# A graph network's edge counts: one-hot products on TensorE in place of one scatter per edge

## The chip, the cores and the metric

The kernel runs on one core of a Trainium2 chip. The core has five engines with instruction streams of their own, which wait for each other through semaphores: TensorE (PE: matrix products, with weight loads shown apart as PEld), VectorE (DVE), ScalarE (ACT), GpSimd (POOL) and SyncE (SP, which here only starts DMAs). Sixteen DMA engines move data between HBM and the on-chip memory SBUF; products land in PSUM. DMAs are started from the queues of SP, ACT and POOL. A POOL DMA may be indirect: a column of indices says which rows it reads or writes. The metric is the device time of one execution in microseconds. A measurement of this kernel can tell about 0.2% from no change.

## The reference

There are 6,250 nodes with 128 features and 106,250 directed edges (`src`, `dst`), sorted by `dst`. Four graph blocks follow each other, each with a residual and a layer norm (`_layernorm(x + block(x))`, in shortened form):

```python
agg = segment_sum(h[src], dst); agg /= maximum(deg, 1)        # block 0, twice (SAGE)
out = agg @ Wl.T + bl + h @ Wr.T
out = segment_sum((x @ W)[src] * (dinv[src] * dinv[dst]), dst)  # block 1 once, block 2 twice (GCN, with loops)
for l in range(3):                                             # block 3: three layers of three hops
    for k in range(1, 4): x_k = segment_sum(x_k1[src] * edge_norm, dst)
```

The nine hops weigh each edge by `edge_weight` and by the weighted degrees of its ends; the other five sums only count edges. What matters here: all these sums run over the same edges, and the first five need, for each pair of a destination and a source, only the number of edges between them.

## The kernel before

Nodes are cut into 49 windows of 128 (`NW`). The kernel makes dense matrices in HBM: `counts`, one byte for each pair of source and destination, 39 MB; and `weights`, four bytes for each pair, for the first 34 windows of destinations or so. Columns (destinations) are grouped into 13 chunks of four or three windows (`SHAPE`, 512 or 384 columns); chunk `c` holds 49 blocks of 128 sources. A sum over edges is then a matrix product: for each block of sources, the block of features is the stationary operand and 128 x 512 counts are the moving one.

The work goes through these stages.

Setup (lines 217 to 358) reads `dst`, `src` and `edge_weight`, spread over partitions; makes a key for each edge from its destination and source; writes `keys`, `recs` (rows of 17 edges) and `edges` to HBM; and decides on tests of the edges' order (`odd`) whether `usual_way` can be taken. The other branch, `general_way`, is for inputs of another shape.

Pass 1 (lines 779 to 821) is the first SAGE layer. For each chunk, it

- fetches rows of 17 x 128 edges (`fetch`), compares each edge's key with its 48 neighbours on both sides to find how often the pair occurs and whether the edge is the first of its pair (`cell`, on DVE), and gets a byte address for each edge;
- scatters one byte for each edge into `counts` (`scatter`, line 588: 17 indirect DMAs for each of 49 blocks), after the chunk has been filled with zeros (`empty`);
- counts degrees by one-hots of 384 places and products (`degrees`, lines 730 to 732), and turns them into the norms (`norms`);
- sums: `counted_sum` (line 479) loads seven blocks of counts at a time (`columns`, line 462), widens them from bytes to 32 bits, in pass 1 on ACT alone (line 501), and multiplies (line 508). Features are split into a high and a low part, so there are two products for each block. For chunks after the first, a second accumulator `half` takes the layer's output for sources that are already done, which is a part of the next layer's sum;
- does the chunk's dense layer (`mean_conv`, `plus_product`), and splits the result for later use.

From chunk 7 on, further parts of the next layer's sums are made ahead (`early_parts`).

Pass 2 (lines 907 to 919) is the second SAGE layer, with the rest of its sums; passes 3 and 4 (lines 940 to 984) are the GCN blocks. Their counts are widened by DVE and ACT in turn. Meanwhile POOL scatters the weights, 35 blocks of 17 indirect DMAs, paced by the products (`Paced`), and then gathers edge records for the last windows (`gathered_edges`). The hops (from line 1253) multiply by `weights` for most chunks and gather rows for the rest, in an order written out by hand.

Up to the hops, the order on each engine comes from a scheduler that follows the program order and the waits. Two orders are forced: `in_line` puts POOL's DMAs behind each other, and SP starts its DMAs in one line, so that a DMA that waits holds those behind it.

The counts' address and value in the lines that the change removes:

```python
nc.vector.tensor_scalar_add(cval[:, i, :], f1[:], 1.0)
...
ins = nc.gpsimd.indirect_dma_start(
    out=mat[:], out_offset=bass.IndirectOffsetOnAxis(ap=celli[:, i, k:k + 1], axis=0),
    in_=vals[:, i, k:k + 1], in_offset=None, **bounds).ins
```

Of the kernel before, what the change touches and what calls it, by code (L numbers as in the profile page):

```python
# [47 lines left out]
P = 128  # L48
# [39 lines left out]

SLOTS, LOADS, STEP, HOTS, GROUP = 30, 12, 2, 5, 4
# [47 lines left out]
def load_weights(nc, a, const, work, ps, ident, tags):  # L137
# [18 lines left out]
    transposed("w1l", a["L0_gnn_W1l"])  # L156
    transposed("w1r", a["L0_gnn_W1r"])
    transposed("w2l", a["L0_gnn_W2l"])
    transposed("w2r", a["L0_gnn_W2r"])
    bcast("b1l", a["L0_gnn_b1l"], D)  # L160
    bcast("b2l", a["L0_gnn_b2l"], D)
# [22 lines left out]
def kernel(ctx: ExitStack, tc: tile.TileContext, a: dict, out: bass.AP):  # L184
# [15 lines left out]
    counts = dram.tile([BASE[NC] + 4 * NB * KD * P, 1], U8, name="counts")  # L200
# [6 lines left out]
    def empty(mats, dt, c, engine):  # L207
        n = 7 * width(c) // (4 if dt == U8 else 16)
        z = zeros[:].bitcast(dt)[:, :n]
        ins = fills[dt, c] = engine.dma_start(  # L210
            mats[BASE[c]:BASE[c + 1]].rearrange("(p s f) o -> p s (f o)", p=P, f=n),
            z.unsqueeze(1).to_broadcast([P, NW * width(c) // n, n])).ins
        tc.declare_no_dep(ins, group=f"cells {dt}", reason="another chunk")
        tc.add_to_no_dep_group(f"cells {dt}", ins)
        return ins

    with tc.tile_pool(name="setup", bufs=1) as setup, \
            tc.tile_pool(name="ps_setup", bufs=2, space=PSUM) as ps:

        def spread(name, ap, dt):  # L220
            t = setup.tile([P, L + 2 * J], dt, name=name)
            nc.sync.dma_start(t[:], bass.AP(ap.tensor, ap.offset, [[L, P], [1, L + 2 * J]]))
            return t
# [4 lines left out]
        dsti = spread("dsti", a["dst"], I32)  # L228
# [3 lines left out]
        main = slice(J, J + L)  # L232


# [3 lines left out]
        nc.vector.tensor_scalar(k1[:], dsti[:], 1023, 13, op0=ALU.bitwise_and, op1=ALU.logical_shift_left)  # L238
        nc.vector.tensor_scalar(k2[:], dsti[:], 20, 23, op0=ALU.logical_shift_right, op1=ALU.logical_shift_left)
# [5 lines left out]
        nc.sync.dma_start(keys[J:].rearrange("(p e) o -> p (e o)", p=P), key[:, main])  # L245


        def field(at):
# [18 lines left out]
        empty(counts, U8, 0, nc.sync)  # L267

# [7 lines left out]
        dst = setup.tile([P, L + 2 * J], F32, name="dst")  # L276
# [6 lines left out]
        nc.vector.tensor_sub(t1[:], dst[:, 2 * J:2 * J + L], dst[:, main])  # L283
        nc.vector.tensor_scalar(t2[:], dst[:, main], float(NOWHERE), None, op0=ALU.is_lt)
        nc.vector.scalar_tensor_tensor(t2[:], t1[:], 0.0, t2[:], op0=ALU.is_equal, op1=ALU.mult)
        nc.vector.tensor_reduce(odd[:, 1:2], t2[:], AX.X, ALU.max)
        nc.vector.tensor_scalar(t2[:], t1[:], float(NOWHERE // 2), None, op0=ALU.is_lt)
        nc.vector.scalar_tensor_tensor(t2[:], t1[:], 1024.0, t2[:], op0=ALU.is_ge, op1=ALU.mult)
        nc.vector.tensor_reduce(odd[:, 2:3], t2[:], AX.X, ALU.max)
# [3 lines left out]
        dmax = setup.tile([P, RPP], F32, name="dmax")  # L293
        nc.vector.tensor_reduce(dmin[:], by_row(dst[:, main]), AX.X, ALU.min)
        nc.vector.tensor_reduce(dmax[:], by_row(dst[:, main]), AX.X, ALU.max)
        rowi = setup.tile([P, RPP], I32, name="rowi")
        nc.gpsimd.iota(rowi[:], pattern=[[1, RPP]], base=0, channel_multiplier=RPP)
        nc.vector.tensor_scalar(rowi[:], rowi[:], ~(P - 1), None, op0=ALU.bitwise_and)
        even = setup.tile([P, RPP], F32, name="even")
        nc.vector.tensor_copy(even[:], rowi[:])  # L300
        d1 = setup.tile([P, RPP], F32, name="d1")
        d2 = setup.tile([P, RPP], F32, name="d2")
        nc.vector.tensor_sub(d1[:], dmax[:], even[:])
        nc.vector.tensor_scalar(d1[:], d1[:], float(2 * P), None, op0=ALU.is_ge)
# [3 lines left out]
        nc.vector.tensor_sub(d2[:], dmin[:], even[:])  # L308
        nc.vector.tensor_scalar(d2[:], d2[:], -float(P), None, op0=ALU.is_lt)
# [6 lines left out]
        row = setup.tile([P, RPP], F32, name="row")  # L316
        nc.gpsimd.iota(row[:], pattern=[[1, RPP]], base=1, channel_multiplier=RPP,
                       allow_small_or_imprecise_dtypes=True)
# [43 lines left out]
    with tc.If(go == 1) as fork:  # L362
        usual_way(tc, a, out, dram, ident, part, first, over, keys, recs, edges, counts, weights, fills, empty)
# [5 lines left out]
def usual_way(ctx, tc, a, out, dram, ident, part, first, over, keys, recs, edges, counts, weights, fills, empty):  # L369
# [9 lines left out]
    iota = const.tile([P, NEAR * P], F16, name="iota")  # L379
    nc.gpsimd.iota(iota[:], pattern=[[1, NEAR * P]], base=0, channel_multiplier=0,  # L380
# [8 lines left out]
    dinvw2 = const.tile([P, NW], F32, name="dinvw2")  # L389

    early_pool = tc.tile_pool(name="early", bufs=1, side="right")
    early = early_pool.__enter__()
    stacked = early.tile([P, DH], F32, name="stacked")
    nc.vector.tensor_add(stacked[:], ident[:, :DH], ident[:, DH:])
    wt = load_weights(nc, a, early, work, ps, ident, ("y", "pp"))

    def new(name, n, d=D):
        return work.tile([P, n, d], F32, name=name, tag=name)


    def table(name, room, dt=F32):
# [1216 lines left out]
```

## Time and profile before

| | us |
|---|---|
| median of 3 runs | 5791.16 (5787.49 to 5791.88) |
| the profiled execution's own time | 5791.37 |
| its span | 5789.5 |
| PE busy | 5254.7 (91%) |
| POOL busy | 4158.4 (72%) |
| DVE busy | 3115.3 (54%) |
| ACT busy | 2141.4 (37%) |
| first product of pass 1 | at 163.46 |
| first product of pass 2 | at 1203.04 |
| first product of the hops | at 2184.53 |

The slices below cut the span into 40 equal parts of 145 us; each digit is the busy share of a slice in tenths, for PEclk the clock that TensorE was granted in tenths of its full speed.

```profile
PE   0656579799999899999999999999999999999998
DVE  7685455258855564444446554444456544444566
ACT  1323346347755442323333323323333333233332
POOL 5777777778877617767767767767777677777775
PEclk9878789899999999999999999999999999999999
DMA  5768785146544449999999999999999999999997
```

Lines of groups read: line of the kernel, engine, operation, what is written and read, its size, the count; then busy time and the mean of one in ns; then the idle time of the engine just before, and what ended it. Lines of waits name who waited for whom, the time in total, how often, and the longest. Lines of the timeline give start and length in us. An engine's busy time does not say that it is the bound of a stage; that is read from what its instructions wait for.

### The profile page before, as it was taken

How to read it: one execution, taken by the hardware profiler on the slowest of the kernel's cores; microseconds unless marked ns; L12 is line 12 of the kernel's file. 1: busy time of each engine (PE TensorE's matmuls, PEld its weight loads, DVE VectorE, ACT ScalarE, POOL GpSimd, SP SyncE). 2: the span in 40 equal slices, each digit the busy share in tenths (PEclk: the TensorE clock that was granted, in tenths of full speed). 3: DMA queues.
4: the chain of work that ended last, by engine and by line, in shares of the span. 5: the costliest groups of instructions: out<-in, count | busy, mean ns of one | idle time of the engine just before them, and what ended most of it. 6: DMA issues, size and time to landing. Idle time of an engine off the chain costs nothing.

```text
span 5789.5 us, 70572 instructions
## 1 busy us (share of the span) xinstructions
PE 5254.7 (91%) x19487; PEld 3143.9 (54%) x19487; DVE 3115.3 (54%) x8828; ACT 2141.4 (37%) x4433; POOL 4158.4 (72%) x4204
## 2 busy tenths in 40 slices
PE   0656579799999899999999999999999999999998
PEld 0334457576788784555555555555555555555455
DVE  7685455258855564444446554444456544444566
ACT  1323346347755442323333323323333333233332
POOL 5777777778877617767767767767777677777775
PEclk9878789899999999999999999999999999999999
DMA  5768785146544449999999999999999999999997
GB/s 184 237 201 248 217 260 154 59 140 177 155 131 137 129 139 333 323 319 325 324 318 310 309 313 323 322 321 323 323 302 312 301 326 324 316 323 324 304 336 264
DMA packets 707889, 1517.46 MB, mean 262 GB/s; under 512 B 153094, under 2 KB 359962, under 8 KB 707226
## 3 DMA queue, kind: packets, MB, share of 16 engines
q1 hardware_dynamic: 524642, 1272.39, 65.1%
q0 software_dynamic: 134080, 180.02, 11.5%
q10 hardware_dynamic: 48760, 60.45, 3.1%
q8 instruction: 155, 2.54, 0.2%
q14 instruction: 252, 2.06, 0.1%
HBM read 1313.22 MB, written 199.20 MB: 261 GB/s over the span
## 4 chain that ended last, share of the span: by engine, by line
PE 71%; DMA 11%; POOL 7%; DVE 6%; issue 4%; ACT 1%; ACTq 0%; SPq 0%; POOLq 0%; DVEq 0%
PE acc L1245 45%; PE acc L508 14%; DMA rows<-stored,gsrc 7%; PE gacc L1212 5%; POOL counts L588 5%; PE pp L435 3%; PE pd L732 1%; DMA cols<-counts 1%; POOL weights L588 1%; PE half L508 1%; DMA slots<-counts 1%; DVE widev L501 1%; DMA counts<-cval,celli 1%; ACT wides L501 1%; POOL rows L1148 1%
## 5 line engine op out<-in xcount | busy, mean ns | idle before, releaser
L1245 PE MATMUL acc<-weighed,hop 128*128 128x512 f32 (+1 forms) x7154 | 3402.6, 591 | 13.2 <-DMA weighed<-weights 6.8
L1148 POOL DMA_INDIRECT rows<-stored,gsrc x2727 | 2614.1, 959 | 981.9 <-issue 347.5
L1195 ACT ACTIVATE both<-rows,gwgt 128x128 fp32r<-128x128 f32 x2718 | 1047.8, 400 | 1969.7 <-DMA rows<-stored,gsrc 1783.5
L1212 PE MATMUL gacc<-both,oh 128*128 128x256 f32 x2718 | 1761.2, 657 | 7.9 <-DVE both L1196 7.9
L1245 PEld LDWEIGHTS acc<-weighed,hop 128*128 128x128 f32 x7154 | 1169.7, 190 | 941.2 <-issue 837.6
L1196 DVE SCALAR_TENSOR_TENSOR both<-rows,gwgt,both 128x128 fp32r<-128x128 f32 x2718 | 923.8, 350 | 1334.1 <-ACT both L1195 1323.6
L508 PE MATMUL acc<-wides,t 128*128 128x512 f32 (+1 forms) x3083 | 875.7, 394 | 359.2 <-ACT wides L501 240.3
L588 POOL DMA_INDIRECT counts<-cval,celli x833 | 828.6, 995 | 263.0 <-issue 245.1
L1212 PEld LDWEIGHTS gacc<-both,oh 128*128 128x128 f32 x2718 | 514.6, 190 | 651.8 <-issue 396.2
L508 PEld LDWEIGHTS acc<-wides,t 128*128 128x128 f32 x3083 | 569.8, 191 | 496.9 <-ACT wides L501 267.1
L588 POOL DMA_INDIRECT weights<-wval,celli x595 | 677.2, 1138 | 181.4 <-issue 167.1
L501 ACT CAST wides<-slots 128x1024 fp32r<-128x1024 uint8 (+3 forms) x684 | 562.3, 862 | 521.5 <-DMA slots<-counts 309.2
L508 PE MATMUL acc<-widev,t 128*128 128x512 f32 (+1 forms) x2044 | 576.8, 390 | 31.5 <-DVE widev L501 27.0
L1175 DVE TENSOR_TENSOR oh<-places,gdst 128x640 fp32r<-128x640 f32 x604 | 473.3, 784 | 213.1 <-PE gacc L1212 212.2
L508 PEld LDWEIGHTS acc<-widev,t 128*128 128x128 f32 x2044 | 376.8, 190 | 112.9 <-DVE widev L501 42.8
L731 DVE TENSOR_SCALAR oh<-iota,dloc 128x384 bf16<-128x384 f16 x833 | 214.2, 320 | 366.8 <-PE pd L732 366.7
L501 ACT CAST wides<-cols 128x1024 fp32r<-128x1024 uint8 (+1 forms) x364 | 285.0, 797 | 298.5 <-DMA cols<-counts 160.7
L501 DVE CAST widev<-cols 128x1024 fp32r<-128x1024 uint8 (+1 forms) x364 | 249.8, 691 | 175.2 <-PE acc L508 137.5
L508 PE MATMUL half<-wides,t 128*128 128x512 f32 (+1 forms) x606 | 188.6, 390 | 0.0
L732 PE MATMUL pd<-oh,lw 128*4 128x384 bf16 x833 | 175.4, 334 | 10.1 <-DVE oh L731 8.1
L501 DVE CAST widev<-slots 128x1024 fp32r<-128x1024 uint8 (+3 forms) x239 | 155.8, 669 | 18.2 <-PE acc L508 13.0
L1065 DVE TENSOR_TENSOR y<-pp,dinvw 128x256 f32<-128x256 f32 (+2 forms) x153 | 82.4, 539 | 139.0 <-PE pp L435 138.7
(266 smaller groups left out, 2790.4 us busy)
## 6 DMA issues: line engine op xcount, KB each, us to landing
weighed<-weights SPq DMA_DIRECT2D x1728, 512.0 KB
weights<-zeros SPq DMA_DIRECT2D x8, 12544.0 KB
slots<-counts SPq DMA_DIRECT2D x174, 448.0 KB
cols<-counts SPq DMA_DIRECT2D x140, 448.0 KB
rows<-stored,gsrc POOLq DMA_INDIRECT x2727
counts<-zeros SPq DMA_DIRECT2D x10, 3136.0 KB
weighed<-weights SPq DMA_DIRECT2D x96, 256.0 KB
stored<-hop ACTq DMA_DIRECT2D x74, 256.0 KB
```

Source lines behind the costliest of these rows:

```text
L435: nc.tensor.matmul(pm[:, j * d:(j + 1) * d], xt[:, j * P:(j + 1) * P], w, start=True, stop=True)
L501: copy(wide[:, :n * cw], t[:, r * cw:(r + n) * cw])
L508: product = nc.tensor.matmul(into[:, :cw], lhs, cols, start=s == begin and i == 0, stop=s == end - 1 and i == len(lhss) - 1).ins
L588: ins = nc.gpsimd.indirect_dma_start(out=mat[:], out_offset=bass.IndirectOffsetOnAxis(ap=celli[:, i, k:k + 1], axis=0), in_=vals[:, i, k:k ...
L731: nc.vector.tensor_scalar(oh[:], iota[:], dloc[:, k:k + 1], None, op0=ALU.is_equal)
L732: nc.tensor.matmul(acc[:], lw[:, k, :], oh[:], start=k == 0, stop=k == KD - 1)
L1148: nc.gpsimd.indirect_dma_start(out=fetched_rows[:, self.slot(self.asked), :], out_offset=None, in_=stored[self.h % 2][:], in_offset=bass.I ...
L1175: nc.vector.tensor_tensor(oh[:, :m, :], places[:].unsqueeze(1).to_broadcast([P, m, P]), gdst[:, i, ks].unsqueeze(2).to_broadcast([P, m, P] ...
L1195: nc.scalar.activation(both[:, :D], x, AF.Copy, scale=w)
L1196: nc.vector.scalar_tensor_tensor(both[:, D:], x, w, both[:, :D].bitcast(F32), op0=ALU.mult, op1=ALU.subtract)
L1212: nc.tensor.matmul(self.acc[:, j * 2 * D:(j + 1) * 2 * D], oh, both, start=k == 0, stop=k == KG - 1)
L1245: nc.tensor.matmul(acc[:, :cw], tables[h][:, s, :], t[:, s % STEP * cw:(s % STEP + 1) * cw], start=s == 0, stop=s == NW - 1)
```

## The change

The matrix of counts is no longer scattered into. The edges are sorted by destination, so the edges of four neighbouring nodes (`G = 4`) lie in one run of at most 128 edges. Setup finds for each four nodes the row of 17 edges where its run begins (`lasts`, `around`, `begin`), and writes `runs`, an overlapping table of 128 keys and 128 edge weights for each row. In pass 1, for each batch of four windows (128 groups), one indirect DMA gathers the runs, one for each partition (`gathered_run`); `prepared` turns keys into a zone (node within the group, source block) and a place (source within the block), transposes them so that edges lie on partitions, and makes the degrees and norms. `building` then makes, for each pair of groups, one-hots of zones (196) and places (128) with one DVE instruction each for eight groups, two products of 128 x 196, and one ACT copy from PSUM into bytes, which writes runs of eight bytes (two groups of four nodes) at a step of 128. A finished window is written to HBM by one DMA.

`building` is a generator. Five windows and one pair are made ahead; after that `Meanwhile` takes 64/49 pairs for each block of sources that `counted_sum` consumes, and in the same way the fills of `weights`, which are now cut into 63 DMAs of 16 pieces for each partition.

Cells are computed only for the 35 blocks that the weights need, at the end of each chunk of pass 1 (three blocks), and their scatters follow at once; `Paced` and the scatter of counts go, as does the counting of degrees. One operand of the cells' comparisons, which was copied to PSUM (`aside`), stays in SBUF. Counts are stored window by window, so a load of seven blocks consists of 896-byte pieces, and the widening copies reorder them. `cols` slots in pass 1 go from seven to five, `wide` buffers from three to two. Weights that only later passes need are loaded after pass 1, and `kept` is allocated there.

```diff
-    def empty(mats, dt, c, engine):
...
+    def empty(c):
+        n = 7 * width(c) // 16
+        mat = weights[BASE[c]:BASE[c + 1]].rearrange("(p s f) o -> p s (f o)", p=P, f=n)
+        fills[c] = []
+        for s in range(0, NW * width(c) // n, 16):
+            ins = nc.sync.dma_start(mat[:, s:s + 16, :], zeros[:, :n].unsqueeze(1).to_broadcast([P, 16, n])).ins
...
+            yield
...
+        nc.scalar.dma_start(lasts[DRIFT:DRIFT + P * RPP].rearrange("(p r) o -> p (r o)", p=P), rowlast[:])
...
+        nc.scalar.dma_start(around[:], bass.AP(lasts.tensor, lasts.offset, [[G, P], [P * G, NBATCH], [1, 2 * DRIFT]]))
+        nc.scalar.dma_start(runs[:, RUN:], bass.AP(a["edge_weight"].tensor, a["edge_weight"].offset + J,
+                                                    [[KD, NW * P], [1, RUN]]))
...
+        for r in (slice(0, 5 * P), slice(5 * P, NW * P)):
+            nc.sync.dma_start(runs[r, :RUN], bass.AP(keys.tensor, keys.offset + J + r.start * KD,
+                                                     [[KD, r.stop - r.start], [1, RUN]]))
...
+    def count_columns(t, c, step, s0):
+        n = SHAPE[c]
+        t = t[:, :n * step * P].rearrange("p (w s f) -> p w s f", s=step, f=P)
+        nc.sync.dma_start(t.rearrange("p w s f -> p w (s f)"), counts[c].rearrange(
+            "(w p f) o -> p w (f o)", w=n, p=P)[:, :, s0 * P:(s0 + step) * P])
+        return t
...
-                copy(wide[:, :n * cw], t[:, r * cw:(r + n) * cw])
+                copy(wide[:, :n * cw].rearrange("p (s w f) -> p s w f", s=n, f=P),
+                     t[:, :, r:r + n, :].rearrange("p w s f -> p s w f"))
...
+            if meanwhile is not None:
+                meanwhile()
...
+        def gathered_run(b):
+
+            t = cells.tile([P, 2 * RUN], F32, name="run", bufs=3)
+            ins = nc.gpsimd.indirect_dma_start(
+                out=t[:], out_offset=None, in_=runs[:],
+                in_offset=bass.IndirectOffsetOnAxis(ap=begin[:, b:b + 1], axis=0)).ins
+            queue.append(in_line(ins))
+            return t
...
+        SOME = 8
+
+        def hot(name, places, spots, k0, n):
+
+            t = hots.tile([P, SOME // 2, n, 2], BF16, name=name)
+            nc.vector.tensor_tensor(
+                t[:], places[:].unsqueeze(1).to_broadcast([P, SOME // 2, n, 2]),
+                spots[:, k0:k0 + SOME].rearrange("p (j o) -> p j o", o=2).unsqueeze(2).to_broadcast(
+                    [P, SOME // 2, n, 2]), op=ALU.is_equal)
+            return t
...
+        def building():
+
+            found, spots = {}, {}
+            found[0] = gathered_run(0)
+            for w in range(NW):
+                b, c = w // WPB, chunk_of(w)
+                if w % WPB == 0:
+                    if b + 1 < NBATCH:
+                        found[b + 1] = gathered_run(b + 1)
+                    spots[b] = prepared(b, found.pop(b))
+                t = spare if w % 2 else cells.tile([P, NW * P], U8, name="built")[:]
+                by_column = t.rearrange("p (s f) -> p s f", f=P)
+                for some in range(GROUPS_W // SOME):
+                    k0 = w % WPB * GROUPS_W + some * SOME
+                    zone = hot("zone", zones2, spots[b], k0, NZ)
+                    place = hot("place", places2, spots[b], P + k0, P)
+                    for pair in range(SOME // 2):
+                        acc = ps_build.tile([P, 2, CW // 2], F32, name="some")
+                        for i in range(2):
+                            nc.tensor.matmul(acc[:, i, :NZ], place[:, pair, :, i], zone[:, pair, :, i],
+                                             start=True, stop=True)
+                        f = some * SOME * G + pair * 2 * G
+                        nc.scalar.copy(by_column[:, :, f:f + 2 * G].rearrange("p s (i d) -> p s i d", d=G),
+                                       acc[:, :, :NZ].rearrange("p i (s d) -> p s i d", d=G))
+                        yield
+                nc.sync.dma_start(counts[c].rearrange("(w p f) o -> w p (f o)", w=SHAPE[c], p=P)[w - START[c]], t)
...
+        meanwhile = Meanwhile()
+        meanwhile.add(building(), 4 * PAIRS_W / NW)
+        meanwhile.some(0, 5 * PAIRS_W + 1)
...
+        meanwhile.add(filling, (ND + 1) * FILLS / (NW * 11))
...
-            fetch_chunk(c + 2)
-            if c + 4 < NC:
-                empty(counts, U8, c + 4, nc.sync)
-            count_cells(c + 1)
-            for i in sorted(i for i in blocks_near(c) if i in degs):
-                degrees(i)
-            norms(c)
...
-            acc = counted_sum(counted, c, both(t0hi, t0lo), [(2, "s")], slots=slots, also=also)
+            acc = counted_sum(counted, c, both(t0hi, t0lo), [(2, "s")], wide_bufs=2, slots=slots, also=also,
+                              meanwhile=meanwhile)
...
-            if c <= ND:
-                empty(weights, F32, c, nc.sync)
+            for i in dense[PER * c:PER * (c + 1)]:
+                filled(chunks_near(i))
+                cell(i, fetch(i))
+        meanwhile.rest()
```

## The prediction

> **What bounds the kernel now.** I read the page's slices first, then the busy time by stage, then the groups and waits of the first stage, then single instructions. The stages come from the timeline: the first product of pass 1 starts at 163.46 us, the first of pass 2 at 1203.04, the first hop product at 2184.53. Busy time in these stretches (columns: stretch, length, busy us and count of PE, weight loads, DVE, ACT, POOL, then granted clock, DMA share, GB/s):
>
> ```profile
> 0.00:163.00 163.00, 2.88 (x7) 1.36 (x7) 103.23 (x323) 15.98 (x26) 92.98 (x104) 1.00 0.55 170
> 163.00:1205.00 1042.00, 755.12 (x3527) 524.26 (x3528) 549.93 (x2119) 439.45 (x586) 797.21 (x804) 0.86 0.63 193
> 1205.00:2180.00 975.00, 924.24 (x4417) 749.83 (x4416) 674.45 (x1640) 529.17 (x760) 654.05 (x570) 0.98 0.52 150
> 2180.00:5789.00 3609.00, 3572.44 (x11538) 1868.49 (x11538) 1787.68 (x4748) 1156.77 (x3062) 2614.12 (x2727) 0.99 0.93 317
> ```
>
> Passes 2 to 4 and the hops are PE's (95% and 99% busy). Pass 1 isn't: PE is at 72% with a clock of 0.86. Its groups and waits, from 40 to 1215 us:
>
> ```profile
> L588 POOL DMA_INDIRECT counts<-cval,celli x833 | 828.6, 995 | 263.0 <-issue 245.1 <-DVE wval L712 9.4 <-DMA counts<-cval,celli 3.7
> L501 ACT CAST wides<-slots 128x1024 fp32r<-128x1024 uint8 x273 | 272.7, 1044 | 380.5 <-DMA slots<-counts 309.2 <-PE half L508 58.2 <-PE acc L508 5.5
> L731 DVE TENSOR_SCALAR oh<-iota,dloc 128x384 bf16<-128x384 f16 x833 | 214.2, 320 | 366.8 <-PE pd L732 366.7
> L732 PE MATMUL pd<-oh,lw 128*4 128x384 bf16 x833 | 175.4, 334 | 10.1 <-DVE oh L731 8.1 <-ACT degT L734 1.7
> L679 DVE TENSOR_TENSOR before<-m,aside 128x816 bf16<-128x816 f32 x48 | 47.7, 994 | 0.1
> L522 ACT COPY agg<-acc 128x512 f32<-128x512 f32 x11 | 6.4, 583 | 9.4 <-PE acc L508 9.4
> L734 ACT COPY degT<-pd 4x384 f32<-4x384 f32 x49 | 22.9, 468 | 159.3 <-PE pd L732 138.2 <-DVE oh L731 19.9 <-DMA slots<-counts 1.2
> L563 DVE TENSOR_TENSOR y<-pp,invdeg 128x384 f32<-128x384 f32 x3 | 1.7, 558 | 1.8 <-PE pp L435 1.8
> ```
>
> The 833 count scatters leave POOL no gap but issue: 828.6 + 263.0 = 1091.6 us, 1.3 us each. ACT waits 309 us for count columns, which are read only when their scatters have landed. So POOL sets pass 1. The scatters end here:
>
> ```profile
> 1124.70 1.04 POOL L588 DMA_INDIRECT counts<-cval,celli  x1 [0.30 <-issue]
> 1126.05 1.07 POOL L588 DMA_INDIRECT counts<-cval,celli  x1 [0.30 <-issue]
> 1127.42 1.00 POOL L588 DMA_INDIRECT weights<-wval,celli  x1 [0.31 <-issue]
> ```
>
> after which the last chunk takes to 1203.
>
> **The change, part by part.** Pass 1 consumes 781 columns of counts ("steps"): 13 chunks of 49, and 144 in the early sums. 81 of 784 build pairs stand ahead of the first step; the rest go at 64/49 = 1.306 a step, so they end after 703/1.306 = 538 steps, in chunk 8. The fills of the weights are spread over the same steps. I price the start, the building steps, the steps after them, and the later passes.
>
> *Start.* Gone: the first count fills, cells and scatters. New: a copy of edge weights and of keys into `runs` (6,272 pieces of 512 B each), the writing and reading back of `lasts`, a gather, `prepared`, 64 pairs before chunk 0 can be read. ACT's queue (60.45 MB, 48,760 packets, 3.1% of 16 engines, so 0.059 us a packet) prices one copy at 6,272/16 x 0.059 = 23 us; `lasts` stands behind it on that queue, and DVE's setup behind `around`. So the branch moves from 34 to about 46 us, the first one-hots to about 53; 16 pairs of one-hots and 64 evictions beside the splits of x take 40; writing and reading back 5 + 4. That is 102; I take 115 for order and queues, and 100 to 163.46 (no gain) as ends.
>
> *ACT in a building step.* Casts: 447 instructions, 389 us by the four forms of L501, over 781 steps 0.50. Evictions, 392 elements from PSUM: L734 (384) 0.468 and L522 (512) 0.583 give 0.475, x 1.306 = 0.62. Short runs can cost more: the writes of single 4-byte cells 12 B apart took 1.35 us for 850 elements (L270), where 17-cell runs took 0.95 (L251). At 1.37 ns an element plus 0.18 an eviction would be 0.72, the upper end; runs of 8 are nearer to the long ones, so 0.475. The rest of ACT (sums, transposes, splits: 53 us) 0.07. Together 1.19.
>
> *DVE.* Gone: L731 (214 us), the degrees' small operations, 14 of 49 cells. New: 196 pairs of one-hots, 1,568 and 1,024 elements, all operands 16-bit. Upper end, by two-source rows (0.682 at 512, 0.994 at 816: 1.03 ns an element): 1.75 + 1.20 = 2.95 a pair. Lower: L731 is the one row with only 16-bit tensors, 0.320 at 384 against 0.558 for the two-source 4-byte form of that size (L563), 0.573 of it: 1.69. I take 1.69 for the type, though L731 has one source. It is 1.69/4 x 1.306 = 0.55 a step. Cells, 35 x 5.6 us (five large at 0.92, ten small at 0.1) over 538: 0.36. `prepared` 11 x 5 us: 0.10; the chunks' ends 0.09. Together 1.10.
>
> The Trainium skill ("VectorE: DVE Perf Modes", The perf-mode tier table) has `tensor_tensor` at twice the rate when everything is bf16 in SBUF, which no row of before shows; with its two elements a cycle the pair would be about 1.65 us and the sum the same within 10 us.
>
> *PE.* Products up to chunk 8: 1,378 at 0.2336 (72 in 16.82 us), narrower ones less: 315 us. Builds: 1,406 at 0.09 (196 of 384 columns of L732, 17 in 2.88 us) to 0.28 (plus L508's 0.19 weight load, unhidden); L435, 128 columns behind a 128x128 load, runs 8 in 1.16, 0.145: I take 0.15, 211 us. L732 goes. Chunk ends 40. 566/538 = 1.05.
>
> *DMA.* Between 800 and 900 us, at 0.98 busy, 295 GB/s moved. Bytes beside the building: fills 112 MB, counts written 35 (the zero fills of counts, 39 MB, go), columns read 35, the rest 15: 197 MB, 670 us, 1.245 a step. The fills come in 1.8 MB parts (6 us each) in SP's queue between count writes and column reads, in place of 12.5 MB at a time; a column read queued behind a part is covered by five slots, an eviction into the second-next `built` by one window's time, 15 us.
>
> *POOL.* 51 weight scatters a chunk at 1.3 us: 1.35 a step. Only the gather of a later run waits behind them in line, with about two chunks of slack; hidden as long as a scatter stays under some 1.8 us. Beside a busy DVE it got longer: 81.86 us for 60 from 1400 to 1500 us, 1.36 each and 0.3 between. The skill ("SBUF — State Buffer", SBUF: two separate sides) speaks against the change: a DVE operation with two SBUF inputs shuts out a GpSimd one that reads SBUF for its whole length, and one-hots and cells now have both inputs in SBUF. If each scatter waited for one 0.97 us one-hot, 2.3 us each would be 2.4 a step; I stay at the row.
>
> *Sum of pass 1.* DMA is the largest, 1.245; ACT, DVE and PE stand close beside it, in fixed orders that wait for each other. Pass 2 to 4 show what such a bound reaches: 865 us of PE work (3,561 products, 80 us of small ones) in 975, 0.89. So 1.245/0.89 = 1.40, x 538 = 753. The 243 steps after have no building: 790 products, 342 of 384 columns at 0.175 and 448 at 0.2336, 165 us, and four chunk ends of 8: 195. Pass 1 ends at 115 + 753 + 195 = 1063 in place of 1203: -140.
>
> *Passes 2 to 4 and hops.* Weight scatters are done about 240 us into pass 2 (187 left of 595), so the one long stall goes:
>
> ```profile
> 1975.93 1.18 PE L508 MATMUL acc<-wides,t 128*128 128x512 f32 x4
> 1991.78 2.07 PE L508 MATMUL acc<-widev,t 128*128 128x512 f32 x4 [14.68 <-DVE widev L501]
> ```
>
> There DVE's casts stood behind gathers behind the last scatters: -14. Columns are read in pieces of 896 B instead of 3,584: some 23 reads lie open at 3.4 us; bounds 0 to +0.9 each, taken +0.2: +4. In the passes with two `cols` buffers a tile takes PE 3.27 us, the cycle of cast and read (1.7 + 3.4)/2 = 2.6: covered up to a read of 4.8; at 5.2 it would cost 0.2 on 182 reads, +36. The late weights load beside the first chunk's products: 0. Hops unchanged: 0. Sum -10.
>
> 5789.5 - 150 = 5639.5 of span, and the 1.9 us that lie around it in that execution (5791.37, against a median of 5791.16): **5641**.
>
> **Rivals.** *All engines overlap almost fully:* start 100, 1.19 a step, chunk ends half hidden: 100 + 640 + 180 = 920, so 5498. For it: the products and builds are data-independent between chunks. Against: chunk ends tie PE, ACT and DVE together.
> *One-hots at the two-source rate (2.95), slower:* DVE 1.10 + 0.41 = 1.51, /0.89 = 1.70, x 538 = 914, start +20, end 1244: +41 - 10, so 5822. It decides from a step of (1203 + 10 - 310)/538 = 1.68. For it: every two-source row of before runs at that rate.
> *Evictions at 0.72:* ACT 1.51, 1.70 a step: about 5816. For it: L270.
> *The count columns' pieces or the casts from four windows slow passes 2 to 4:* +36 to +100, 5680 to 5740 with the gain of pass 1.
> *The built path isn't taken:* dst and the edges' runs in the reference's inputs stay inside the new limits (drift of -2 to 21 rows against 48), so no.
>
> **How the numbers follow.** My case (5540 to 5740, passes 2 to 4 a little slower included) 0.63; near full overlap 0.17; one-hots slow 0.12; evictions slow 0.08, a part of which the drift of the step could still hold at no change. Measurement tells 0.2% (12 us) apart. Faster 0.63 + 0.17 - 0.02 = 0.78, same 0.04, slower 0.18. The range, 5500 to 5820, leaves out about half of the fast and of the slow cases.
>
> **What would show it.** Right: no count scatters, 595 + 13 indirect DMAs on POOL ahead of the edge gathers; pass 2 starting near 1060; a zone one-hot near 1.0 us and a place near 0.7; evictions near 0.475; DMA share above 0.85 up to chunk 8; the 14.68 us stall gone. Wrong: zone at 1.75; evictions above 0.7; scatters above 1.8 with one-hots waiting for a gathered run; column reads above 4.8 us in passes 3 and 4; DVE casts of 1,024 above 0.69.

## The result, and the profile after

The changed kernel takes 5844.94 us (median of 4 runs, 5842.29 to 5850.64) beside 5790.8 us for the kernel before: a ratio of 1.0096, with an interval of 1.0078 to 1.0113. It is slower by about 1%, clear of what a measurement can tell, where I had forecast 5641 and a gain. The profiled execution took 5842.29 us with a span of 5840.4.

The busy slices of the changed kernel's page (145 us each, tenths):

```profile
PE   4646456889999999999999999999999999999999
DVE  7646355628955664444446654444456544444566
ACT  5646456755855443332333323333333333333332
POOL 0654644760000015776767767767777677777775
PEclk9878778999999999999999999999999999999999
DMA  8756656445644558999999999999999899999997
```

From the second to the seventh slice no engine is busy throughout: PE, DVE, ACT, POOL and DMA all stand at three to seven tenths. Sevens alone do not clear an engine: before the change POOL showed sevens all through pass 1 and was its bound, since the rest of its time there was issue, 0.30 us between one scatter and the next. But now POOL too falls to four to six, so the engines seem to take turns waiting. The waits have to show it. The stages, cut at the first product of each (pass 1 at 122.98 us, pass 2 at 1292.57, the steady hop products at 2240.08; columns as before: stretch, length, PE, weight loads, DVE, ACT, POOL, clock, DMA share, GB/s):

```profile
0.00:123.00 123.00, 44.87 (x195) 26.17 (x195) 83.51 (x192) 55.27 (x113) 11.19 (x26) 1.00 0.84 276
123.00:1292.00 1169.00, 771.67 (x4068) 540.14 (x4069) 592.18 (x1312) 693.81 (x1235) 664.60 (x607) 0.85 0.58 174
1292.00:2240.00 948.00, 905.33 (x4407) 747.43 (x4405) 654.28 (x1635) 525.73 (x759) 33.44 (x33) 0.99 0.55 154
2240.00:5840.00 3600.00, 3564.71 (x11538) 1862.09 (x11538) 1786.04 (x4747) 1161.94 (x3062) 2612.26 (x2727) 1.00 0.93 317
```

Pass 2 starts 89.5 us later than before (1292.6 against 1203.0). Passes 2 to 4 take 947.5 us in place of 981.5, 34.0 less; the hops 4.7 less. 89.5 - 34.0 - 4.7 = 50.8, the whole difference of the spans. So the loss lies ahead of pass 2. Pass 1 starts 40.5 us sooner than before (122.98 against 163.46) and still ends 89.5 later, and its waits name the reason. First DVE's, then POOL's (that one from 200 to 900 us):

```profile
DVE ki L760 <- DMA run<-runs,begin: 323.5, 8, 43.8
DVE zone L812 <- PE some L848: 56.9, 62, 3.2
```

```profile
POOL weights L630 <- DVE low L737: 121.8, 4, 31.1
POOL weights L630 <- DVE f L719: 41.0, 1, 41.0
POOL weights L630 <- DVE celli L738: 23.2, 1, 23.2
```

Eight times DVE waits at L760, the first instruction of `prepared`, for a gathered run, 323.5 us in all; and POOL, which issues the gathers, waits for DVE's cells in turn. One round of it in the timeline, POOL first and then DVE:

```profile
422.41 0.98 POOL L630 DMA_INDIRECT weights<-wval,celli  x1 [0.30 <-issue]
423.70 0.99 POOL L748 DMA_INDIRECT run<-runs,begin  x1 [0.31 <-issue]
454.38 1.68 POOL L630 DMA_INDIRECT weights<-wval,celli  x1 [29.68 <-DVE low L737]
```

```profile
426.50 0.23 DVE L760 CAST ki<-run 128x128 int32<-128x128 f32 x1 [35.55 <-DMA run<-runs,begin]
```

The gather at 423.70 is POOL's next instruction after 51 scatters without a pause. Its run lands at 426.5 and DVE goes on after 35.6 us of nothing. Then DVE needs 28 us until the next block's cells are done (454.38), POOL scatters 51 times up to its next gather at 523.83 (69.4 us, 1.36 us each), the gathered run lands 3 us later, and DVE is waiting again. 28 + 69 + 3 is 100, and a chunk of pass 1 takes 100.5 (L607's multiplication, once a chunk, moves from 171.1 to 874.4 in seven chunks). The loop is the bound; the granted clock falls with it, to 0.79 to 0.84 between 200 and 800 us.

### The profile page after: what moved, and what is told of

Its sections match the earlier page's. It is cut to its first block, busy times and chain, and to the rows that moved or that the text cites. A ratio compares the mean times of both kernels' runs of the same rounds, so it can differ in the third digit from the quotient of the medians.

```text
span 5840.4 us, 70939 instructions
## 1 busy us (share of the span) xinstructions
PE 5286.6 (91%) x20205; PEld 3175.8 (54%) x20205; DVE 3116.0 (53%) x7884; ACT 2436.8 (42%) x5168; POOL 3321.5 (57%) x3393
## 4 chain that ended last, share of the span: by engine, by line
PE 57%; DMA 18%; issue 8%; DVE 7%; POOL 6%; ACT 4%; ACTq 0%; POOLq 0%; SPq 0%; DVEq 0%
PE acc L1361 36%; DMA rows<-stored,gsrc 14%; PE acc L552 11%; POOL weights L630 5%; PE gacc L1328 4%; PE pp L467 3%; ACT wides L544 2%; DMA cols<-counts 2%; POOL rows L1264 1%; PE half L552 1%; DVE widev L544 1%; DVE both L1312 1%; ACT both L1311 1%; DVE zone L812 1%; PE some L848 1%
## 5 line engine op out<-in xcount | busy, mean ns | idle before, releaser
L552 PE MATMUL acc<-wides,t 128*128 128x512 f32 (+1 forms) x3083 | 976.0, 408 | 63.1 <-ACT wides L544 56.5
L630 POOL DMA_INDIRECT weights<-wval,celli x595 | 653.6, 1098 | 549.6 <-DVE celli L738 208.3
L544 ACT CAST wides<-slots 128x1024 fp32r<-128x1024 uint8 (+3 forms) x684 | 592.5, 881 | 224.9 <-PE half L552 87.3
L1291 DVE TENSOR_TENSOR oh<-places,gdst 128x640 fp32r<-128x640 f32 x604 | 473.0, 783 | 187.9 <-PE gacc L1328 186.9
L848 PE MATMUL some<-zone,place 128*128 128x196 bf16 x1568 | 273.6, 269 | 301.3 <-DVE place L812 280.3
L986 POOL DMA_INDIRECT gm<-recs,gat x17 | 17.6, 1035 | 880.6 <-DVE gwgt L1003 878.0
L848 PEld LDWEIGHTS <-place 128*128 128x128 bf16 x1568 | 117.5, 104 | 449.1 <-DVE place L812 285.9
L851 ACT CAST built<-some 128x392 uint8<-128x392 f32 x400 | 185.4, 521 | 167.4 <-PE some L848 165.1
L851 ACT CAST slots<-some 128x392 uint8<-128x392 f32 x384 | 177.5, 513 | 141.6 <-PE some L848 137.2
L812 DVE TENSOR_TENSOR zone<-zones,spots 128x1568 bf16<-128x1568 bf16 x196 | 190.0, 969 | 58.0 <-PE some L848 56.9
```

The lines of the kernel that those rows point to most:

```text
L544: copy(wide[:, :n * cw].rearrange("p (s w f) -> p s w f", s=n, f=P), t[:, :, r:r + n, :].rearrange("p w s f -> p s w f"))
L552: nc.tensor.matmul(into[:, :cw], lhs, cols, start=s == begin and i == 0, stop=s == end - 1 and i == len(lhss) - 1)
L630: ins = nc.gpsimd.indirect_dma_start(out=weights[:], out_offset=bass.IndirectOffsetOnAxis(ap=celli[:, i, k:k + 1], axis=0), in_=wval[:, i, ...
L812: nc.vector.tensor_tensor(t[:], places[:].unsqueeze(1).to_broadcast([P, SOME // 2, n, 2]), spots[:, k0:k0 + SOME].rearrange("p (j o) -> p ...
L848: nc.tensor.matmul(acc[:, i, :NZ], place[:, pair, :, i], zone[:, pair, :, i], start=True, stop=True)
L851: nc.scalar.copy(by_column[:, :, f:f + 2 * G].rearrange("p s (i d) -> p s i d", d=G), acc[:, :, :NZ].rearrange("p i (s d) -> p s i d", d=G))
```

## The experiments

**Chips.** The runs fell on several chips, and these are of two kinds. On some, as on the chip of the result, before takes 5788 to 5796 us. On others it takes 7800 to 7913 us, and the changed kernel 6927. In the experiments a kernel is compared with kernels on the same kind of chip. What differs is told at the end of this section. Where a chunk is given, it is the mean of chunks 1 to 7 of pass 1, from the starts of L607's multiplication.

**The run gathered earlier.** My theory after the result: the place of the gather in POOL's line makes the loss. The edit of the run with six buffers (`e1`; `c2`, `c3` and `c4` are the same kernel):

```diff
-            t = cells.tile([P, 2 * RUN], F32, name="run", bufs=3)
+            t = cells.tile([P, 2 * RUN], F32, name="run", bufs=6)
...
-            found[0] = gathered_run(0)
+            for b in range(4):
+                found[b] = gathered_run(b)
...
-                    if b + 1 < NBATCH:
-                        found[b + 1] = gathered_run(b + 1)
+                    if b + 4 < NBATCH:
+                        found[b + 4] = gathered_run(b + 4)
```

With four buffers (`e2`, `c5`) two runs are gathered ahead, and then `b + 2`. In what follows, "theory" is this account, and "rival" is another one that an experiment could bring out.

> The gather of each run is issued one batch earlier (four buffers in place of three), so it stands in front of 51 more weight scatters in POOL's queue. Theory (the loss is DVE's in-line read of a run whose gather stands behind 51 scatters, eight stalls of 33 to 44 us, 324 us in all): the waits of L760 go, a chunk of pass 1 takes 60 to 68 us in place of 100 (its running part is 60; POOL's 51 scatters and one gather are 51 x 1.29 + 2.8 = 68), and the time is 5844 - 8 x (32 to 41) = 5516 to 5590. Rival A (the engines share ports and DMA so that a step costs 1.40 us, my sum): a chunk 69 plus its end, about 5640. Rival B (DVE or POOL are late for another reason, the cells for instance, and the run is only what the wait shows): 5780 to 5850.

> The same with six buffers: each run is gathered three batches earlier. Theory: no stall is left that one batch did not already take, so within 20 us of the run with one batch earlier. If the first of the two leaves a part of the stalls (DVE's order could read the run still earlier), this one takes it, and is the faster by that part.

Both were on a chip of the slower kind (before 7800). Four buffers: 6911 us, 0.8842 of before [0.8797, 0.8888], a chunk of 103.0. Six buffers: 6861, 0.8797 [0.8748, 0.8845], 94.1. With four buffers L760 still waited three times in pass 1, 95.7 us in all. The built order says why: DVE's read of a run moved forward with the gather. Most runs had been read 1.25 to 1.44 batches ahead of their own one-hots, and were now read 2.25 to 2.44 ahead, so the batch of lead was used up at once. Six buffers leave the read at 2.3 to 2.5. With them the waits of L760 went, but pauses of 15 to 36 us stood in their place, for which the profile names no engine of this core; some of them ended as POOL's burst of scatters ended. By my numbers the theory had missed, and a control had to say whether the chip was to blame.

> The changed kernel once more, beside the runs of the next two: 1.010 of the time of before by the first measurement, with the eight stalls of DVE at L760. If the chip of the first experiments (where before took 7800 us) treats the two kernels differently, the ratio here says it.

> The run gathered three batches earlier, on the chip of the control. Theory (in-line read of a late run): no stall of L760, the changed kernel's time less 8 x (32 to 41) us, 5516 to 5590 where it is 5844, ratio to before 0.953 to 0.966. Rival A (a step costs 1.40 us once nothing waits): 5640. Rival B (the stall only moves to another wait, for instance the cells' scatters or column reads): over 5750.

On a second chip of that kind (before 7825) the changed kernel took 6927 us, 0.8856 of before [0.8834, 0.8879]: on this kind of chip the change is a gain of 11%, and the earlier gathers bring only 0.4% more (6892, 0.8816 [0.8794, 0.8838]; chunks 103.5 and 95.1). Between the late gather and the burst of scatters itself these chips could not decide.

**Half the scatters.** `range(0, KD, 2)` in place of `range(KD)` in `scatter`.

> Nine of the 17 scatters of every block of weights are issued, eight are left out (the weights lack those cells); the order is that of the changed kernel. A chunk then has 27 scatters. Theory: the gather comes 24 x 1.29 = 31 us sooner in each chunk, eight stalls fall from 33 to 44 us to 2 to 13, and the time falls by about 8 x 31 = 247 to some 5600. Rival (the gather is late by itself or for its indices): no change of the stalls, the time within 20 us of 5844.

6619 us, 0.8473 [0.8419, 0.8526], on a slower chip; the changed kernel with all its scatters gave 0.8856 on another of that kind. L760's waits fell from 25 to 44 us to 11 to 22, where I had expected 2 to 13, and the chunk from 103.5 to 78.4. So the scatters ahead of the gather set the wait's length, but half a burst would shorten it by either account.

**Cells and scatters behind the building**, on top of the six buffers:

```diff
-            for i in dense[PER * c:PER * (c + 1)]:
+            for i in dense[7 * max(c - 8, 0):7 * max(c - 7, 0)]:
```

> The run three batches earlier, and the cells of the weights with their 595 scatters not three blocks a chunk from chunk 0 on, but seven blocks a chunk in chunks 8 to 12, behind all 13 gathers in POOL's line. Theory (bursts of 51 scatters in POOL's line, and what waits behind them, make a chunk 100 us): the chunks 0 to 7 take 57 to 66 us each, and building ends near 650 us. Rival (a building step costs 1.40 us or more by the engines' own work and DMA): 69 us or more, building ends after 850 us. The scatters' 767 us then run to about 1450, beside pass 2, and what they cost there is seen in pass 2's chunks.

The chunks without a scatter take 58.8 us, within the theory's 57 to 66, even on a slower chip (before 7888). Building ends at 750 us, between the theory's 650 and the rival's 850. The window of chunks 1 to 7:

```profile
181.00:593.00 412.00, 373.84 (x2102) 244.62 (x2100) 246.50 (x451) 368.54 (x694) 3.55 (x3) 0.99 1.02 324
```

PE is at 91%, ACT at 89%, and the profile's DMA share at 1.02 with 324 GB/s. This is what the building costs when neither scatters nor the cells' work on DVE (246.5 us busy here, 335.1 in the whole kernel's same window below) stand beside it: 1.20 us a step. Afterwards, with 595 scatters in one stream that ended at 1507 us, one chunk alone took 442 us. The whole was 7059 us, 0.895 [0.8914, 0.8985], slower than the same gathers with the cells in their old place on that chip, which is the next run.

> The run three batches earlier once more. On the two chips so far (before 7800 and 7825 us) the waits of L760 went, and pauses of the same length, ended by the end of a burst of scatters and by no semaphore that the profile shows, stood in their place. On a chip where before takes 5791 us and transfers move beside a burst: chunks of 60 to 68 us and 5516 to 5590 us, if the late run is the cause; over 5750 if the burst itself is.

The chip was of the slower kind again: 6950 us, 0.8811 [0.875, 0.8873].

**POOL busy without scatters.** To part the line from the burst, each scatter is replaced by work of POOL's own, so the line is long and no burst of indirect DMAs runs.

```diff
-            ins = nc.gpsimd.indirect_dma_start(
-                out=weights[:], out_offset=..., in_=wval[:, i, k:k + 1], ...).ins
+            ins = nc.gpsimd.tensor_copy(spent[:], wval[:, i, k // 3:k // 3 + 1].to_broadcast([P, 350])).ins
```

> The changed kernel's order, but in place of each of the 595 scatters into the weights POOL does three copies of 350 elements in SBUF (the weights lack all their cells), estimated from the memsets of 224 and 304 elements (0.28 and 0.34 us) at 3 x 0.44 = 1.3 us, the length of one scatter. So POOL's line is as long as before and no burst of indirect DMAs runs. Theory (the run's gather stands behind 51 entries of POOL's line, and DVE reads it in line): the waits of L760 stay, eight of 30 to 45 us, a chunk takes 95 to 105 us. Rival (the burst of indirect DMAs itself holds transfers or instructions up, and L760 is only where it shows): the waits of L760 shrink under 10 us and a chunk takes 60 to 68 us.

> The same POOL work, and the run gathered two batches earlier (five buffers). Theory: no wait of L760, a chunk of 60 to 68 us (59 us is what a chunk takes in the run with the cells behind the building, before any scatter; POOL's 51 entries are 66 us, so it may be POOL that sets 66 to 68), and building ends 250 to 300 us earlier than with the late gathers. Rival: no difference between these two runs.

5984.57 and 5981.77 us (before 5787.8): no difference, as the rival had it, but for a reason of my making. The copies took 0.62 us on average in place of 0.38:

```profile
L630 POOL COPY spent<-wval 128x350 f32<-128x350 f32 x1785 | 1110.9, 622 | 237.2 <-DVE wval L739 127.8
```

So 153 of them and their gaps are at least 104 us a batch, POOL's line was full, and the chunk was 99 us with either order. Nothing follows for the gather. With one iota of 208 elements for each scatter (`nc.gpsimd.iota(spent[:], pattern=[[1, 104], [0, 2]], ...)`, held back until the cells are done) the length is right. The weights lack their cells here too:

> The changed kernel's order, with one iota of 208 elements in place of each of the 595 scatters into the weights (which lack all their cells): from the iota of 256 (1.54 us) an estimated 1.25 us and 0.06 between, 1.3 us. No burst of indirect DMAs. Theory (the gather's place in POOL's line): seven or eight waits of L760 of 30 to 45 us stay, a chunk of pass 1 takes 95 to 105 us. Rival (the burst itself): the waits go, 60 to 68 us.

> The same with the runs gathered three batches earlier (six buffers). Theory: no wait of L760 in the first six chunks, a chunk of 60 to 68 us (59 is the undisturbed chunk, 66 POOL's 51 iotas), building ends 250 to 300 us earlier than with the late gathers. Rival: no difference between these two runs.

The iotas took 1.25 us. DVE's waits with the late gather, and then those with the earlier one:

```profile
DVE ki L758 <- DMA run<-runs,begin: 343.3, 8, 49.0
```

```profile
DVE cols L537 <- DMA cols<-counts: 186.9, 1, 186.9
DVE zone L810 <- PE some L847: 55.5, 56, 2.6
```

6016 us against 5698 (before 5796), chunks of 103.7 and 62.7 us: without any burst of scatters the late gather alone makes eight pauses, and the earlier gather takes all of them away, 318.7 us. Building ends 333 us sooner, a little more than the 250 to 300 expected. The rival falls. (In both, a read of columns late in pass 1 waits for POOL's last iotas, 163.5 and 186.9 us, which the changed kernel does not have; so their chunks are to be compared, and their difference, and not their times with before.)

**The whole kernel with the earlier gathers**, on the same chip:

> The whole kernel with the runs gathered three batches earlier, correct in all parts. On a chip where before takes 5790 us: theory 5516 to 5600, ratio 0.953 to 0.967; rival (the burst itself) 5750 to 5850. On a chip where before takes 7800: 0.88, as measured three times.

5543.24 us (4 runs, 5533.18 to 5550.48), 0.9568 of before [0.9552, 0.9584]: inside the theory's 5516 to 5600, and faster than both kernels. Its stages:

```profile
0.00:124.00 124.00, 44.78 (x194) 26.09 (x194) 83.02 (x190) 54.73 (x112) 13.96 (x29) 1.00 0.85 275
124.00:995.00 871.00, 758.17 (x4071) 529.26 (x4071) 589.86 (x1314) 691.61 (x1236) 673.10 (x560) 0.97 0.78 234
995.00:1935.00 940.00, 900.39 (x4405) 742.58 (x4403) 655.84 (x1634) 526.16 (x759) 82.21 (x78) 1.00 0.55 155
1935.00:5531.00 3596.00, 3564.87 (x11538) 1863.53 (x11538) 1788.34 (x4747) 1160.83 (x3062) 2608.88 (x2727) 1.00 0.93 317
```

Pass 1 does the work of the changed kernel (758 us of PE, 590 of DVE, 692 of ACT, 673 of POOL) in 871 us in place of 1169, and the clock is 0.97 in place of 0.85. Chunks 1 to 7 of it alone, and what is left of the wait (4.9 us of it in the setup):

```profile
181.00:593.00 412.00, 363.12 (x2009) 241.37 (x2008) 335.12 (x724) 353.41 (x661) 330.67 (x267) 0.98 0.98 299
```

```profile
DVE ki L760 <- DMA run<-runs,begin: 28.0, 3, 19.5
```

POOL is now slower than the chunk: 51 scatters take it about 80 us a batch (gathers at 317.1, 398.5, 477.8, 558.2), a chunk takes 61.9, so the lead shrinks from 41 us at the tenth run (gathered 398.5, read 439.4) to 6.5 at the last. Three batches are barely enough, and one of them goes to the read's own move forward, which the built order shows here as with four buffers (2.3 to 2.5 batches ahead of use).

**One batch earlier, twice the fills, fewer scatters a chunk.** The last runs asked how far ahead the gather must be and whether DMA sets the 61.9 us. Each fill was doubled by a second DMA of the same size into memory that nothing reads; for the last kernel the blocks of cells go two and three a chunk in turn and the fills over `NW * 14` steps in place of `NW * 11`.

> The run three batches earlier, and every fill of the weights (63 DMAs of 1.8 MB) issued a second time, into memory that nothing reads: 113 MB more in SP's queue beside the building. If DMA is the bound of a building step, as my sum had it (1.245 us a step at 295 GB/s), pass 1 gets longer by 113 MB / 295 GB/s = 383 us, nearly all of it. If the engines' chain bounds it and DMA has 35% to spare, by less than 100 us.

> The run one batch earlier (four buffers). Where transfers move beside scatters: POOL's line of 80 us a batch against a chunk of 61 eats one batch's lead in about three chunks; then DVE waits at L760 again, some 20 us a chunk in chunks 4 to 8. Between the two: 5600 to 5700. If one batch's lead were enough, 5540 to 5560; if it did nothing, 5840.

> Runs three batches earlier and every fill twice, 113 MB more. DMA at 299 GB/s and 0.98 in chunks 1 to 7 there: if it is the bound, 113 MB / 299 GB/s = 378 us more, 5900 to 5930 in all. If it isn't, under 100 more.

> The runs three batches earlier; two or three blocks of cells a chunk in turn (23 by chunk 8 in place of 27), three in the last four chunks, and the fills spread over 14 chunks of steps in place of 11. By the DMA term: 12.5 MB x (9/11 - 9/14) = 2.2 MB less a chunk, 7 us of 61 at 299 GB/s, and POOL's line 42 scatters of 1.5 us = 66 us a batch in place of 80. If DMA sets the chunk: 55 to 58 us a chunk in place of 61, 20 to 50 us in all less than the run three batches earlier (ratio to before 0.948 to 0.953 where that has 0.957). If the fixed order of PE, ACT and DVE sets it: within 10 us of that run.

> The runs three batches earlier, 23 blocks of cells by chunk 8 in place of 27 and the fills over 14 chunks of steps in place of 11, once more. Where before takes 5790 us: if DMA sets the chunk, 55 to 58 us a chunk and a ratio of 0.948 to 0.953; if the order of PE, ACT and DVE sets it, 0.955 to 0.959 as with the early gathers alone. Where before takes 7800: 0.878, as measured.

All five fell on the slower kind of chip: 0.9138 [0.9105, 0.9171] and 0.9123 [0.9059, 0.9186] with the fills twice (chunks 125.5 and 121.3), 0.8822 [0.8763, 0.888] with four buffers (99.1), 0.8783 [0.8741, 0.8826] and 0.8796 [0.877, 0.8822] with the spread (91.0 and 93.0). With four buffers six waits of L760 stayed in pass 1 on this chip, 228.9 us in all. Twice the fills lengthened 6892 us to 7145, about 250 us, on a chip where the pauses still leave DMA idle; that lies between the two ends that I had given and decides neither. How far ahead the gather must be, and whether DMA or the order of the engines sets the chunk, stays open for the chip of the result.

> The kernel before with a profile on this chip. Where it takes 7800 us, the 2010 us above the first chip's time stand where POOL streams indirect DMAs without a pause: pass 1 (833 count scatters), the 595 weight scatters in pass 2 and the gathers of the hops; in passes 3 and 4 without scatters the two chips agree within 1%.

**What differs between the chips.** Before took 7890.85 us in this run; its steady hop products start at 3361.0 us in place of 2184.5 and take 4528 us in place of 3605. The changed kernel on another slower chip: 2436.1 and 4504. So the change takes 925 us off the part ahead of the hops there, and next to nothing off the hops, whose gathers it leaves alone. My expectation for passes 3 and 4 could not be read in this run, since its scatters go on until 2909 us; in the changed kernel, from the 26th chunk end to the hops, where no scatter runs, the kinds of chip agree (812 us and 816). The same kernel, the same stretch, with POOL scattering all through it, on the chip of the result and then on the slower one:

```profile
1034.00:1280.00 246.00, 224.33 (x1085) 174.33 (x1084) 88.62 (x222) 162.64 (x232) 192.17 (x179) 0.99 0.36 102
```

```profile
1034.00:1280.00 246.00, 107.38 (x517) 77.69 (x515) 93.35 (x229) 86.76 (x156) 189.11 (x169) 0.69 0.21 58
```

POOL is as busy on both, PE half as busy on the second, and DMA moves 58 GB/s in place of 102. The run with the cells behind the building adds the counterpart: on a slower chip, with no scatter beside it, a chunk took 58.8 us. So on the second kind other work lost about half its pace in this stretch, while a stream of indirect DMAs ran. Why some chips do so is not shown.

## Why the prediction was wrong

**The step that failed is POOL's.** I wrote that only the gather of a later run waits behind the scatters in line, "with about two chunks of slack", and costed it at nothing. I had counted the slack from the text: gather `b + 1` is written where batch `b` begins, and building runs 81 pairs ahead. But the place that counts is where DVE reads the run, and the built order has that far ahead of the use: run 5 is read when the one-hots of 3.56 batches have been made, 1.44 batches before its own. The text issues that gather where batch 4 begins, so in DVE's order the read stands ahead of the place in the text where the gather is issued. And the 51 scatters in front of the gather wait for cells that stand behind that same read on DVE. Together it is a loop, and I had listed the gather among the signs of a wrong forecast only for scatters above 1.8 us; at 1.36 it was enough. The term that I had put at nothing measured 323.5 us of waits. With the gather moved, 5543 in place of 5845 (before 5796 and 5791): the step cost about 300 us. The forecast without it was 98 us too slow, 68 of them in pass 1 (its end at 995 against 1063).

**Rivals.** None of mine was the one that came. The slower one, one-hots at 2.95 us a pair, was not it; a rival with this mechanism (51 x 1.36 + 3 + 28 us up to DVE's next cells, a chunk of 100) could have been worked out from the order. The case of nearly full overlap (5498) was nearer to the kernel without the loop than my main one.

**The terms,** from the groups of the changed kernel in pass 1:

```profile
L630 POOL DMA_INDIRECT weights<-wval,celli x595 | 653.6, 1098 | 549.6 <-DVE celli L738 208.3 <-issue 175.6 <-DVE low L737 121.8
L848 PE MATMUL some<-zone,place 128*128 128x196 bf16 x1568 | 273.6, 269 | 301.3 <-DVE place L812 280.3 <-ACT built L851 8.6 <-ACT slots L851 5.8
L812 DVE TENSOR_TENSOR zone<-zones,spots 128x1568 bf16<-128x1568 bf16 x196 | 190.0, 969 | 58.0 <-PE some L848 56.9
L851 ACT CAST built<-some 128x392 uint8<-128x392 f32 x400 | 185.4, 521 | 167.4 <-PE some L848 165.1
L812 DVE TENSOR_TENSOR place<-places,spots 128x1024 bf16<-128x1024 bf16 x196 | 133.7, 682 | 0.0
```

- One-hots: 0.969 + 0.682 = 1.651 us a pair against 1.69 taken from the 16-bit row. Right; the 2.95 of the two-source rows was not. The Trainium skill ("VectorE: DVE Perf Modes", The perf-mode tier table) has twice the rate for bf16 operands in SBUF; the estimate from it was 1.65, and these rows agree.
- Evictions: 0.521 and 0.513 us each against 0.475, far from the 0.72 of the upper end; in a step that is 0.52 x 1.306 = 0.68 against 0.62. Builds: 273.6/1568 = 0.174 of busy PE against 0.15.
- Start: the first product at 123 against 115. Right.
- A building step: in the run with the earlier gathers, the building steps go from the first product at 124.6 to the last one-hot at 774.1 us, 649.5/538 = 1.21 us against my 1.40. The work was sized well (DMA 1.245 at 295 GB/s); the factor 0.89 for engines that wait for each other was not. DMA at 0.98 of its time and 299 GB/s in chunks 1 to 7, beside PE at 88% and ACT at 86%, shows nearly none of that loss. But 324 GB/s moved in the run without scatters beside the building, so 299 need not be DMA's limit; that DMA sets the step is only argued. The steps after the building took 221 us against 195.
- Passes 2 to 4: -34 against -10. The stall of 14.68 us went as forecast; PE's waits for DVE's casts there, before and after:

```profile
PE acc L508 <- DVE widev L501: 27.0, 30, 14.7
```

```profile
PE acc L552 <- DVE widev L544: 12.3, 27, 2.2
```

The column reads in short pieces cost nothing that can be seen (ACT's casts of 1,024 wait 121.8 us for them in place of 133.4). The rest is PE's busy time, 905 in place of 926 us, which I had not counted; the clock at 0.99 in place of 0.98 makes some 9 of these 21, the others I can't place.
- The Trainium skill's warning ("SBUF — State Buffer", SBUF: two separate sides), that a DVE operation with two SBUF inputs shuts a GpSimd one out while it runs, agrees with the single instructions of the changed kernel. A scatter took 0.98 us where DVE was idle (352 of the 595). Where it began under a one-hot, it took the longer the more of the one-hot was left: 1.18 us with 0.2 to 0.4 us left, 1.36 with 0.4 to 0.6, 1.58 with 0.6 to 0.8 (medians). Under a reduction, which has one input, it stayed at 0.98. Two scatters of POOL, and the DVE instructions that ran as they began:

```profile
353.45 1.61 POOL L630 DMA_INDIRECT weights<-wval,celli  x1 [0.30 <-issue]
355.36 0.98 POOL L630 DMA_INDIRECT weights<-wval,celli  x1 [0.30 <-issue]
```

```profile
353.26 0.94 DVE L812 TENSOR_TENSOR zone<-zones,spots 128x1568 bf16<-128x1568 bf16 x1
354.86 0.99 DVE L715 TENSOR_REDUCE f<-before 128x17 f32<-128x816 bf16 x1
```

The first ends 0.86 us after the one-hot does. So such a scatter waits for what is left of the one-hot, and the mean of all 595 was 1.10 us. The 2.3 us each did not come, since not every scatter met a one-hot at its start.

## What to carry to other kernels

An item that is moved onto an in-order queue is late when its first reader comes to it in that engine's built order, not when its result is needed; look up that place, and what stands ahead of the item, before calling its slack. Where what stands ahead waits in turn for the reader's engine, add up the round trip, since it bounds the stage even if no engine is busy. Here the sign of such a loop was that every engine stood at about half with the clock down. Moving the gather, with three more buffers, was worth more than the change itself: 5845 became 5543. The built order has to be read again after such a move, since the reader can move forward with the item.

## What the runs showed of the hardware

- The two kinds of chip: 5790 and 7800 to 7913 us for one program, and a change of +1% on the one that is -11% on the other. The verdict on this change holds for the kind of chip it was taken on.
- POOL and DVE slow each other down where both read SBUF. Beside POOL's copies in SBUF the one-hots took 1.085 and 0.915 us in place of 0.969 and 0.682:

```profile
L809 DVE TENSOR_TENSOR zone<-zones,spots 128x1568 bf16<-128x1568 bf16 x78 | 84.6, 1085 | 24.8 <-PE some L845 24.7
L809 DVE TENSOR_TENSOR place<-places,spots 128x1024 bf16<-128x1024 bf16 x78 | 71.4, 915 | 0.0
```

and POOL's copies of 350 elements took 0.48 us where DVE was idle and 0.82 where DVE was busy for nine tenths of the copy. POOL's iotas, which read nothing from SBUF, took 1.25 us either way, and the one-hots beside them stayed at 0.97 and 0.69.
- The granted clock was lower where PE waited: 0.85 over pass 1 with the loop and 0.97 without it, for the same products.
